# The first stage of an attention kernel put in a fixed order, with query and key halves sent through DRAM

## The chip, the cores and the metric

The kernel runs on one core of one Trainium2 chip. The metric is the device time of one execution in microseconds (us). A core has five engines that run side by side and wait for one another with semaphores: TensorE (PE) for matrix products, VectorE (DVE), ScalarE (ACT) and GpSimd (POOL) for elementwise work, and SyncE (SP), which here does nothing but issue transfers (DMAs). [...] A DMA belongs to the queue of the engine that issues it.

## The reference, cut to what matters

The input has two sequences of 2048 tokens with 256 features. Four layers follow one another, each added to its input: a softmax attention, a gated mixing of features, a second attention without softmax, and the mixing again. Only the first, `_L0_attn_a_ref`, is touched by the change, and what is computed stays the same:

```python
x = L0_attn_a_x                       # (2, 2048, 256)
h = layernorm(x)
q = h @ Wq + bq                       # 16 heads of 16
k = h @ Wk + bk                       # 4 key heads of 16
v = h @ Wv + bv
scores = einsum('bghnd,bhsd->bghns', q, k)      # 4 groups x 4 key heads
attn = softmax(scores / SCALE)        # SCALE = 4
out = einsum('bghns,bhsd->bghnd', attn, v)
x = x + out @ Wo + bo
```

## The kernel before, in words

The 4096 tokens lie in eight blocks of 512 (`NB = 8`), four for each sequence. `load(j)` prepares one block: it normalizes the tokens, turns them (`turn`, eight PE transposes), and makes keys (`pk`), queries (`pq`, two products of 128 rows, m = 0 and 1) and values (`pv`). Queries go to `qT`, values to `vA`, both with the bias already added.

Score products take their operands in a shorter float format. So that nothing is lost, each key and query is split into a high half (`kh`, `qh`: a cast) and a low half (what the cast left over: `kf`, `ql`, a subtraction on POOL). Keys and queries of one head, with their halves, are laid out over 64 partitions, so that one product sums all combinations. Laying them out is the task of `spread`: sixteen DMAs of 16 rows and 32 KB each, from SBUF to SBUF, for one block of keys (`kP`) or for one unit's queries (`qP`). For the first blocks it uses the queues of SP, POOL and ACT in turn.

A unit is one block of queries with one of four groups: 32 units of 16 key blocks (kb) of 128 keys. `project(u)` casts the query halves for two units at a time (when g is even) and lays them out. There are two `qh` and two `ql` buffers, and three sets of `qP`.

The softmax needs the largest score of each row before it can form exponentials, so `largest()` runs ahead: 64 steps for each unit, in each step one product of 128 x 512 scores (L300) and one maximum over it on DVE (L304). The look-ahead leads by `LEAD = 64 + 16` steps when the main loop begins. After a unit's 64 steps `turn_maxima` transposes the maxima and sends them to `mrows`.

The main loop then does for each key block: four look-ahead steps, four score products (L477), four products that subtract the maximum (L481), four exponentials on ACT (L485), and the four products with the values of the key block before (L464). `finish` closes a unit: sums and outputs go through DMAs (L385 to L395), DVE inverts the sums (L392), and after four units the output product is added to the tokens. There too the output bias is added to the tokens, on POOL (L378, once for each block of tokens).

What is in the program's text between the start and the main loop is not kept in that order. A scheduler places the instructions on each engine by its own estimate of when they can run; an instruction with nothing to wait for may move far ahead. `spaced` and the round counter in the text only decide in which order the instructions are offered to it. Later stages of the kernel use a helper, `in_order`, that ties each instruction to the one before it on its engine.

## Time and profile before

| | us |
|---|---|
| median of three runs (2225.53 to 2232.43) | 2229.49 |
| profiled execution | 2234.2 |
| its span, first to last instruction | 2232.1 |
| PE busy in it | 2171.0 |
| DVE busy in it | 1736.7 |
| ACT busy in it | 1421.4 |
| POOL busy in it | 361.4 |
| mean granted clock of PE | 0.987 |

An engine is busy while it executes an instruction; waiting, and issuing DMAs from SP and ACT, does not count. PE's products overlap, so a busy PE is not a PE at its peak. The granted clock is the share of full speed that the chip allows PE. A wait is put down to the engine or DMA whose signal came last.

### The profile page before, as it was taken

The page shows a single profiled execution, that of the slowest core. Times are in us where ns is not written, and L with a number is a line of the kernel's source. Part 1 is how long each engine was busy: PE and PEld are TensorE (multiplying, and loading weights), DVE is VectorE, ACT ScalarE, POOL GpSimd, SP SyncE. Part 2 cuts the span into 40 slices and gives each one's busy share as a digit, 9 for nine tenths or more (in the row PEclk, how much of TensorE's full clock was granted, in tenths as well). Part 3 has the DMA queues.
Part 4 walks back from the last instruction along what each step waited for, and adds up shares of the span by engine and source line. Part 5 has one row for each costly group of instructions (what it writes and reads, how often), then busy time and mean ns, then how long its engine had stood idle before and what let it go on. Part 6 is the DMA issues. An engine that isn't in the chain of part 4 may idle for free.

```text
span 2232.1 us, 39785 instructions
## 1 busy us (share of the span) xinstructions
PE 2171.0 (97%) x14426; PEld 1047.4 (47%) x14426; DVE 1736.7 (78%) x3339; ACT 1421.4 (64%) x2746; POOL 361.4 (16%) x337
## 2 busy tenths in 40 slices
PE   5999999999999999999999999999999999999998
PEld 2444444444444444444444444444343567676434
DVE  6758998988898899889889889989135588886335
ACT  2137777777777777777777777777864444554442
POOL 6310000000000000000000000000036245541450
PEclk9889999999999999999999999999999999999999
DMA  5111000100011000110001000100100000000002
GB/s 145 34 26 54 16 20 20 23 16 16 16 23 24 16 16 19 23 22 16 16 22 25 17 16 17 25 20 6 46 5 1 1 1 1 2 1 1 0 0 76
DMA packets 49779, 47.29 MB, mean 21 GB/s; under 512 B 25264, under 2 KB 34224, under 8 KB 49328
## 3 DMA queue, kind: packets, MB, share of 16 engines
q1 hardware_dynamic: 46944, 41.93, 7.8%
q8 instruction: 114, 1.87, 0.4%
q10 hardware_dynamic: 1360, 1.91, 0.3%
q0 software_dynamic: 1280, 0.92, 0.2%
q14 instruction: 81, 0.66, 0.1%
HBM read 14.29 MB, written 4.72 MB: 9 GB/s over the span
## 4 chain that ended last, share of the span: by engine, by line
PE 84%; DVE 7%; SPq 3%; DMA 1%; ACT 1%; issue 1%; POOL 1%; ACTq 0%; DVEq 0%; POOLq 0%
PE av L464 20%; PE s L300 17%; PE p L477 11%; PE q1f L653 7%; PE p L481 7%; DVE mx L304 4%; PE q2f L663 4%; PE pe L941 2%; PE po L407 1%; PE bpo L967 1%; SPq L389 1%; PE pw L811 1%; PE pq L254 1%; PE pq L802 1%; PE pv L811 1%; SPq L216 1%
## 5 line engine op out<-in xcount | busy, mean ns | idle before, releaser
L304 DVE TENSOR_REDUCE mx<-s 128x1 f32<-128x512 f32 x2048 | 1274.4, 684 | 135.5 <-PE s L300 131.8
L485 ACT ACTIVATE e<-p 128x512 f32<-128x512 f32 x2048 | 1061.3, 605 | 364.2 <-PE p L481 357.3
L300 PE MATMUL s<-a_kP,qP 64*128 64x512 f32 x2048 | 724.5, 473 | 16.2 <-DVE mx L304 14.3
L481 PE MATMUL p<-a_m,a_pick 64*128 64x512 f32 x2048 | 590.5, 418 | 0.0
L300 PEld LDWEIGHTS s<-a_kP,qP 64*128 64x128 f32 x2048 | 290.1, 185 | 587.4 <-DVE mx L304 552.1
L464 PE MATMUL av<-e,a_v 128*32 128x512 f32 x4096 | 548.0, 606 | 0.0
L477 PE MATMUL p<-qP,a_kP 64*128 64x512 f32 x2048 | 534.5, 398 | 2.0 <-ACT e L485 1.9
L477 PEld LDWEIGHTS p<-qP,a_kP 64*128 64x128 f32 x2048 | 287.7, 186 | 54.7 <-ACT e L485 27.0
L481 PEld LDWEIGHTS p<-a_m,a_pick 64*128 64x128 f32 x2048 | 285.0, 185 | 41.5 <-issue 3.0
L653 PE MATMUL q1f<-zq,wf 128*128 128x512 f32 x384 | 175.5, 600 | 0.0
L401 POOL TENSOR_TENSOR oc<-oc,sums 128x512 f32<-128x512 f32 x16 | 20.6, 1286 | 807.2 <-DMA sums<-dr 567.2
L464 PEld LDWEIGHTS av<-e,a_v 128*32 128x32 f32 x4096 | 81.0, 108 | 128.9 <-issue 120.3
L654 ACT ACTIVATE a1f<-q1f,wf 128x512 f32<-128x512 f32 x96 | 66.0, 689 | 99.5 <-PE q1f L653 96.1
L653 PEld LDWEIGHTS q1f<-zq,wf 128*128 128x128 f32 x384 | 70.6, 190 | 98.0 <-issue 86.4
L280 POOL TENSOR_TENSOR ql<-zq,qh 128x512 f32<-128x512 f32 x16 | 20.4, 1278 | 471.8 <-DMA dr<-rs 295.3
L663 PE MATMUL q2f<-a1f,wf 128*128 128x512 f32 x192 | 90.7, 617 | 0.0
L947 DVE TENSOR_TENSOR en<-pe,small 128x512 f32<-128x512 f32 x128 | 79.4, 683 | 12.3 <-PE pe L941 12.0
L692 DVE TENSOR_SCALAR cf<-cf,f_beta,alphaf 128x512 f32<-128x512 f32 x32 | 33.6, 1051 | 53.9 <-ACT cf L691 53.7
L696 POOL TENSOR_TENSOR tf<-cf,zq 128x512 f32<-128x512 f32 x32 | 56.1, 1752 | 93.6 <-DVE cf L692 93.2
L665 ACT ACTIVATE a2f<-q2f,wf 128x512 f32<-128x512 f32 x48 | 32.7, 688 | 56.0 <-PE q2f L663 56.0
L663 PEld LDWEIGHTS q2f<-a1f,wf 128*128 128x128 f32 x192 | 35.8, 196 | 45.9 <-issue 44.9
L698 POOL TENSOR_TENSOR zq<-zq,tf 128x512 f32<-128x512 f32 x32 | 56.8, 1775 | 2.5
(187 smaller groups left out, 1712.7 us busy)
## 6 DMA issues: line engine op xcount, KB each, us to landing
qP<-qh SPq DMA_DIRECT2D x256, 32.0 KB
qP<-ql SPq DMA_DIRECT2D x248, 32.0 KB
xs<-in_x SPq DMA_DIRECT2D x8, 512.0 KB
oc<-avs SPq DMA_DIRECT2D x128, 32.0 KB
sums<-dr SPq DMA_DIRECT2D x128, 32.0 KB
out<-xs SPq DMA_DIRECT2D x16, 256.0 KB
a_m<-mr SPq DMA_DIRECT2D x128, 4.0 KB
rope<-in_const SPq DMA_DIRECT2D x1, 2048.0 KB
```

The source lines that it names most:

```text
L300: mm(s, qP[r // 2][row, qi * P : (qi + 1) * P], kP[r // 2][row, k0 + kb * BLK : k0 + (kb + 1) * BLK], start=True, stop=True,)
L304: nc.vector.tensor_reduce(mx[:, qi, r : r + 1, kb], s, AX.X, ALU.max)
L464: mm(av[32 * r : 32 * r + 32, :], vA[:, units[u][0] // BPB * KB + kb, 32 * r : 32 * r + 32], es[r], start=(kb == 0), stop=(kb == KB - 1),)
L477: mm(t[r], kP[r // 2][row, k0 : k0 + P], qP[r // 2][row, :], start=True, stop=False)
L481: mm(t[r], pick[row, :], mrow[r // 2][row, :], start=False, stop=True)
L485: nc.scalar.activation(es[r], t[r], AF.Exp, scale=1.0 / HD**0.5)
L653: mm(q1, w1[:, c, m * P : (m + 1) * P], z[:, c, :], start=(c == 0), stop=(c == 1))
L654: nc.scalar.activation(a1[:, m, :], q1, AF.Gelu, bias=b1[:, m : m + 1])
L663: mm(q2, w2[:, c, :], a1[:, c, :], start=(c == 0), stop=(c == 1))
L696: nc.gpsimd.tensor_tensor(t1, cs, z[:, 0, :], ALU.mult)
L698: nc.gpsimd.tensor_tensor(z[:, 1, :], z[:, 1, :], t1, ALU.subtract)
L947: nc.vector.tensor_tensor(self.ens[t][w], pes[w].rearrange("p (h n) -> p h n", h=4), const("triu").unsqueeze(1).to_broadcast([P, 4, P]), A ...
```

## The change

1. Everything from the start to the end of the lead is listed step by step, and `in_order` ties all five engines, SP included, to that order. `spaced` and the rounds are gone. Blocks 0 and 1 are taken as far as the first queries and keys, then `pieces` hands out what is left of the blocks, one piece after every third look-ahead step, and later one for each key block of the main loop instead of every second.
2. `spread` is gone. `stored` writes the two halves to a DRAM tile in four DMAs (each half twice), with the rows in the order in which they are needed, and `fetch` reads two tiles of 128 rows from it. For queries four writes serve two units (256 KB each). All are issued by SP. For block 0 the halves are made by DVE straight from PSUM (`halve`), also for the first queries.
3. Value weights are packed without gaps (64 columns instead of 128). The value tile is set to 1.0 by POOL beforehand and ACT copies the values into it. The value bias is folded into the row that is added to the tokens (`bo_row`).
4. Loads: the constants come in three pieces, the token blocks 4 to 7 are issued after the first queries, and key and query biases are loaded by SP. The statistics of a block (`look`) are separate from its normalization, which moves from DVE to ACT (`scale`).
5. Two in five look-ahead steps of unit 0 take their PSUM bank from the other pool. The addition of `bo_row` to the tokens is kept at its place in the program.

The diff, cut to its core:

```diff
+    def in_order(first, which=(engines.PE, engines.DVE, engines.Activation, engines.Pool)):
+        last = {}
+        for ins in nc.cur_bb.bb.instructions[first:]:
+            if ins.engine in which:
+                if ins.engine in last:
+                    tc.add_manual_dep(
...
+                last[ins.engine] = ins
...
             def rows():
...
                 for of, e, to in heads:
                     nc.sync.dma_start(wo[to : to + 16, :, :], dwo[of : of + 16, :, e, :])
+                    at = _WA["bv"][0] + of
+                    nc.sync.dma_start(bv[to : to + 16, :], wa_d[0:1, at : at + 16].rearrange("o p -> p o"))
                 nc.sync.dma_start(bo, wa_d[:, slice(*_WA["bo"])])
+                yield
...
-            def spread(to, of, queues):
-                n = 0
-                for r in range(KV):
-                    for c, half in enumerate(of):
-                        at = 64 * (r % 2) + 16 * c
-                        queues[n % len(queues)].dma_start(
-                            to[r // 2][at : at + 16, :].bitcast(F32), half[16 * r : 16 * r + 16, :]
-                        )
-                        n += 1
+            def halve(hi, lo, product, bias):
+                if product is None:
+                    nc.vector.tensor_copy(hi, lo)
+                    nc.gpsimd.tensor_tensor(lo, lo, hi.bitcast(F32), ALU.subtract)
+                else:
+                    nc.vector.tensor_scalar(hi, product, bias, None, ALU.add)
+                    nc.vector.scalar_tensor_tensor(lo, product, bias, hi.bitcast(F32), ALU.add, ALU.subtract)
+                return lo
+
+            def stored(parts, rows, order):
+                d = dram.tile([4 * rows, BLK], F32, tag=f"d{rows}", name=f"d{rows}")
+                for at, i in enumerate(order):
+                    nc.sync.dma_start(d.rearrange("(p a) n -> p a n", a=4)[:, at, :], parts[i].bitcast(F32))
+                return d
+
+            def fetch(to, d, first):
+                for p in range(2):
+                    nc.sync.dma_start(to[p].bitcast(F32), d[first + P * p : first + P * (p + 1), :])
...
+            def look(j):
+                looks[j] = scales(lambda t: xs[:, 4 * j + t, :], f"a{j}")
+
+            def load(j, ld):
                 z = ld.tile([P, 4, D], F32, tag="z", name=f"z{j}")
-                normalize(z, lambda t: xs[:, 4 * j + t, :], f"a{j}")
-                yield
+                scale(z, lambda t: xs[:, 4 * j + t, :], *looks.pop(j))
...
+                kl = halve(kh, kf, pk[0:64, :] if j == 0 else None, bk)
+                d = stored((kh, kl), 64, (0, 0, 1, 1))
+                fetch([kP[p][:, j * BLK : (j + 1) * BLK] for p in range(2)], d, 0)
                 yield
...
+                        mm(
+                            pv[:, t * 64 : (t + 1) * 64], zb[c][:, t * P : (t + 1) * P], wv[:, c, :],
+                            start=(c == 0), stop=(c == 1),
+                        )
+                nc.scalar.copy(
...
             def project(u):
                 j, g = units[u]
                 if g % 2 == 0:
+                    if u > 0:
+                        qf = qT[:, g // 2, j * BLK : (j + 1) * BLK]
+                        qh = sb.tile([P, BLK], F32R, tag="qh", name=f"qh{u}", bufs=2)
+                        nc.vector.tensor_copy(qh, qf)
+                        ql = sb.tile([P, BLK], F32, tag="ql", name=f"ql{u}", bufs=2)
+                        nc.gpsimd.tensor_tensor(ql, qf, qh.bitcast(F32), ALU.subtract)
+                        halves[j] = qh, ql
+                    halves[j] = stored(halves[j], P, (0, 1, 0, 1))
                 qP = [sb.tile([P, BLK], F32R, tag=f"qP{p}", name=f"qP{u}_{p}", bufs=3) for p in range(2)]
-                spread(qP, [t[rows_g, :] for t in halves[j] * 2], [nc.sync, nc.gpsimd] if u == 0 else [nc.sync])
+                fetch(qP, halves[j], 2 * P * (g % 2))
...
+                        pool, tag = (psp, "p") if first and (4 * qi + r) % 5 > 2 else (pss, "s")
...
+                    tc.keep_in_program_order(
+                        nc.gpsimd.tensor_tensor(
+                            tokens(j), tokens(j), bo_row.unsqueeze(1).to_broadcast([P, 4, D]), ALU.add
+                        )
+                    )
...
+            arrive(0)
...
+            for r in range(KV):
+                nc.sync.dma_start(bk[16 * r : 16 * r + 16, :], wa_d[32 * r : 32 * r + 16, slice(*_WA["bk"])])
+            arrive(1)
...
+            arrive(2)
+            arrive(3)
+            blocks = [load(j, ld) for j in range(NB)]
+            look(0)
+            compact(wk, wkb, nc.scalar.copy)
+            look(1)
+            next(blocks[0])
+            compact(wq, wqb, nc.vector.tensor_copy)
+            next(blocks[0])
+            next(blocks[0])
+            project(0)
+            next(blocks[1])
+            next(blocks[1])
+            look(2)
+            look(3)
+            project(1)
+            at = slice(P, _CONST["mhalf"][0])
+            nc.sync.dma_start(small[:, at], consts[:, at])
+            for j in range(BPB, NB):
+                arrive(j)
+            compact(wv, wvb, nc.vector.tensor_copy)
+            more = rows()
+            next(more)
+
+            def memsets():
...
+                for j in range(NB):
+                    nc.gpsimd.memset(vA[:, 4 * j : 4 * j + 4, :], 1.0)
+
+            def pieces():
+                for j in (2, 3):
+                    for _ in range(2):
+                        next(blocks[j])
+                        yield
+                memsets()
+                look(4)
+                for j in range(BPB):
+                    for _ in blocks[j]:
+                        yield
+                for j in range(BPB, NB):
+                    if j + 1 < NB:
+                        look(j + 1)
+                    for _ in blocks[j]:
+                        yield
+                    if j == BPB:
+                        next(more)
+
+            rest = pieces()
+            LEAD = 64 + 16
+            for n in range(LEAD):
                 next(ahead)
+                if n % 3 == 1:
                     next(rest, None)
+                for f in later:
+                    f()
+                later.clear()
+            in_order(begin, (engines.PE, engines.DVE, engines.Activation, engines.Pool, engines.SP))
...
-                if kb % 2 == 0 and rest is not None and next(rest, "end") == "end":
+                if rest is not None and next(rest, "end") == "end":
```

## The prediction

> **What bounds the kernel now.** I read the page first (share of the span, slices), then the waits of TensorE (PE), then the start of the run in the windows and the timeline, because the change lies there.
>
> ```profile
> span 2232.1 us, 39785 instructions
> ...
> PE 2171.0 (97%) x14426; PEld 1047.4 (47%) x14426; DVE 1736.7 (78%) x3339; ACT 1421.4 (64%) x2746; POOL 361.4 (16%) x337
> ...
> PE   5999999999999999999999999999999999999998
> ...
> PEclk9889999999999999999999999999999999999999
> ```
>
> PE is busy 97% of the span. Time can come only from PE's work, its 61 us of idle time, or stretches at a lower granted clock. The clock row shows such a stretch in slices 2 and 3.
>
> ```profile
> 80.00:90.00 10.00, 8.76 (x23) 2.93 (x22) 8.63 (x15) 1.47 (x3) 2.54 (x2) 1.00 0.06 13
> 90.00:100.00 10.00, 7.13 (x15) 3.38 (x15) 10.00 (x12) 0.00 (x0) 10.00 (x5) 0.50 0.03 7
> 100.00:120.00 20.00, 19.41 (x58) 9.49 (x57) 12.74 (x26) 3.70 (x7) 5.32 (x3) 0.74 0.11 23
> 120.00:140.00 20.00, 18.48 (x56) 8.11 (x54) 17.59 (x32) 3.54 (x6) 4.87 (x3) 0.86 0.14 31
> 140.00:160.00 20.00, 19.95 (x97) 9.61 (x95) 3.12 (x6) 10.46 (x20) 2.55 (x2) 0.80 0.12 25
> ```
>
> The columns are PE, weight loads, DVE, ACT and POOL busy, clock, DMA share, GB/s. From 90 to 160 us the clock is 0.50, 0.74, 0.86, 0.80. At two states, full and half, that is 10 + 10.4 + 5.6 + 8 = 34 us at half rate, or 17 us lost where PE has work. The timeline (start, duration) shows what precedes it:
>
> ```profile
> 38.77 0.49 PE L300 MATMUL s<-a_kP,qP 64*128 64x512 f32 x1
> ...
> 87.46 11.88 POOL L378 TENSOR_TENSOR xs<-xs,a_bo_row 128x1024 f32<-128x1024 f32 x5 [18.85 <-DVE a_bo_row L207]
> ...
> 94.79 6.29 DVE L130 TENSOR_SCALAR z<-xs,mv_a,rs_a 128x256 f32<-128x256 f32 x4
> ...
> 197.96 0.40 PE L477 MATMUL p<-qP,a_kP 64*128 64x512 f32 x2
> ```
>
> The first score step of the look-ahead is at 38.8 us. At 87 us five of the eight bias additions of L378 run on POOL, long before they are needed, and beside them four normalizations take 6.29 us, which take 1.4 us elsewhere (timeline). PE waits, the clock falls. Unit 1 of the main loop begins at 197.96 us; I call all before it the front. The waits of PE in the front and in the main loop (198 to 1600 us) are, in us in all, times, longest:
>
> ```profile
> PE tr L137 <- DVE z L130: 23.9, 4, 20.6
> PE pv L262 <- ACT zq L255: 3.0, 2, 2.6
> PE s L300 <- DVE mx L304: 2.0, 4, 1.0
> ...
> PE s L300 <- DVE mx L304: 12.3, 36, 1.3
> ```
>
> So the front's 198 us are 20.6 of start, 8.3 of later waits, 17 of half rate, and the rest, 152, is PE work at full clock. In the main loop an undisturbed key block takes 2.71 us in the timeline, of which four reductions on DVE take 2.48; PE stalls only where DVE is held up.
>
> **The change, part by part.**
>
> *Start of the front.* Tokens 0 arrive at about 5 us in both. Statistics: 1.4 + 0.37 + 0.3 us on DVE, 1.2 on POOL, then four scalings on ACT (0.6, then 0.5 each, from L367), last at 10.3. Transposes and their copies end at 11.7, the key product at about 14.5, its halves (two DVE passes of 0.7 from PSUM) at 16. Before, DVE walked through the statistics of all eight blocks first (15 to 20 us) and PE began at 20.6. Then the halves go through DRAM. A write to DRAM and its landing is seen here:
>
> ```profile
> 210.27 0.52 SPq L393 DMA_DIRECT2D dr<-rs  x1
> 211.91 1.72 SPq L395 DMA_DIRECT2D sums<-dr  x4
> ```
>
> The reader of dr is issued 1.64 us after its writer. The page "DMA: Bandwidth & Descriptors" of the Trainium skill (Anatomy of one DMA) speaks against the change: a fixed 2.0 us for each DMA plus bytes over 436 GB/s, heaviest to HBM, so two in series cost twice what one does. By the row the trip costs 1.64 plus the data (the outputs at the end write 125 GB/s at a 0.37 share, so some 340 GB/s when full), by the rule 0.4 us more for each leg. SP issues keys (4 writes, 2 reads), then queries (4 writes, 2 reads), about 0.6 us each, each read waiting for its writes. By the rows: keys written by 18.6, read by 22; queries written by 25, read by 28.5 to 29.5; by the rule 1.6 us later. I take 29.5 for the first step: 9 us earlier than 38.8. But PE does only blocks 0 and 1 meanwhile: two transposes (1.03 each), two key products (1.93), one query product (1.9), 7.8 us of work. Its idle start is 29.5 - 7.8 = 21.7 us, against 20.6 now: the start itself gains nothing.
>
> *From the first step to unit 1.* The same 152 us of PE work. Value products have 64 instead of 128 columns, but each keeps its weight load (0.12 us; eight matmuls of two passes are 2.05 us now, at least 1.86 then): minus 1. DVE loses the normalizations (32, 17.9 us) and the value additions (8 x 0.685), and gets the query casts of all units: listing ends at the lead, so the scheduler pulls project's casts (L307) forward as soon as qT is there; in the built order nine stand before the main loop and six in its first eight key blocks, 0.43 each, up to 1.44 beside POOL. For the 80 lead steps DVE has 80 x 0.62 + four looks x 2.1 + casts, halves and bias 8 = 66 us, PE 75: PE is the longer. The eight additions of L378 stay at their place in the main loop, where reductions ran beside them at 4.87/8 = 0.61 us, so undisturbed: cost nothing; without that cover 8 x 2.4 = 19 us. The scalings on ACT (8 x 2.1 us) and the value copies lie in ACT's idle time (41.6 us before zb alone); ACT and POOL no longer issue key pieces, so ACT's waits for those (10.3 us before zq) and PE's 3.0 behind them go. On POOL the mask memsets (4 x 0.52) and eight new ones of the value tile (at most as long each, by their size) come after the key halves of block 3, some 6.5 us, against about six steps until the first value copy needs them: just covered, and within the 8 us of waits taken below where not. Two in five steps of unit 0 use the four banks of the other pool, so DVE can fall further behind before PE stops. Blocks 6 and 7 finish at one piece for each key block instead of every second; the weights of the later stages load sooner, and nobody waits for them.
>
> *What queues.* All transfers go through SP in order, and eight completion semaphores in rotation make each issue wait for the eighth before it. The key writes of block 2 stand behind seventeen small loads of Wo, bv and bo and the last 2 MB of tokens; 4-byte rows like these took 5 us to land. I get the keys of block 2 at about 58 us, needed for step 32 at about 57: a small wait. A cast needs the buffer of the cast before the last, freed when four 256 KB writes have landed: 1.28 (POOL half) + 2 (issue) + 1.64 + 0.75, some 6.5 us, longer behind a key read. Casts come every 4 us on average, two buffers allow 8; where two or three stand close, DVE stops, with the reductions behind it, and PE after three banks. Bounds: 0 to 20 us of PE idle; I take 8 with the waits of looks and key reads.
>
> *Clock.* "TensorE: Matmul & The Clock Gate" (What's actually happening) says that one busy window of 3.4 us restores full rate. The row shows PE dense from 101 us and 0.74 for the whole of 100 to 120, so half rate for 10 us more. By the rule an idle stretch costs PE under 2 us, by the row 5 to 10. I follow the row: 17 us are there to be won, and one new stall longer than a window would take back 5 to 10. I keep 3.
>
> Sum of the front: 21.7 + 151 + 8 + 3 = 184, against 198: minus 14. Bounds: no waits beyond 4 and full clock, 177; 15 of waits and 15 of half rate, 204.
>
> *Main loop after unit 1.* Before, each unit's sixteen 32 KB query pieces take SP 10 us, and the softmax sums queue between them. DVE, in order, waits for both:
>
> ```profile
> DVE rs L392 <- DMA rs<-ds: 27.7, 15, 17.9
> ...
> DVE qh L278 <- issue: 3.1, 8, 0.7
> DVE mx L304 <- PE p L477: 2.2, 2, 1.1
> DVE qh L278 <- DMA qP<-qh: 1.9, 3, 1.2
> ```
>
> Without the single 17.9, at the end where DVE has no reductions, that is 9.8 + 5 us, and each cast adds 0.34. PE lost 12.3 to reductions that came late. Now the casts are gone from here and two reads replace sixteen pieces, so the sums leave at once. I take 11 of the 12.3; bounds 4 (another DMA becomes late) and 12.3. The work behind attention is untouched.
>
> Together minus 25. The profiled execution took 2234.2 us (span 2232.1 and 2.1 around it): 2209. The median of the runs is 4.7 lower, 2229.5; from there 2204.5, so I say 2205.
>
> **Rivals.**
> *Casts choke the lead (slower).* The casts' buffers and SP's order decide: with twelve casts at 4 us spacing and two buffers, the cover ends at 8 us from cast to landing. Each us beyond it costs 12 x 0.5 = 6 us. At 12.5 us (a key read of 3 us and its writes stand before each set, landing near 2 us) that is 27 and the gain is gone; at 15 us it is 42: 2247. For it: SP's single order and sixteen new sets of 1 MB (four times 128 rows of 2 KB). Against: DMA share was 0.1 to 0.4. Chance 0.08.
> *Only the main loop gains.* The front keeps stalling: half rate comes back with a stall at block 2 or at a cast; front 194 to 200, main loop minus 11: about 2217. Chance 0.22.
> *The front runs clean.* 177 and the full 12.3: 2196. Chance 0.25.
> *Nothing to see.* The reads of 512 KB delay the sums as the pieces did and the front gains little: within 6 us. Chance 0.06.
>
> **How the numbers follow.** Chances: main case 0.39 (2198 to 2211), clean 0.25, main loop alone 0.22, nothing 0.06, slower 0.08. A measurement of this kernel tells about 0.3%, 6.7 us, from no change. The three gaining cases give 0.86 faster, 0.06 the same, 0.08 slower. The range 2189 to 2223 takes in the clean case and the main loop alone with their spread, and leaves out the last two and a little.
>
> **What would show it.** First L332 step at 29.5 us, not 38.8. Unit 1 beginning near 184 us. Clock 0.9 or more between 60 and 160 us; no additions of L411 before the main loop. DVE's waits for rs (L426) and for query casts after 180 us near zero, and PE's wait for reductions there under 2 us. I am wrong if DVE waits at L307 for more than 15 us in all, if PE waits for keys of block 2 or 3, or if the first step comes later than 34 us.

## The result, and the profile after

The kernel after takes 2191.86 us (median of 4 runs, 2187.96 to 2195.94) against 2227.91 us before: ratio 0.9836, 95% interval 0.9808 to 0.9864. Measured a second time on another occasion (`e10_after_again` below), the ratio was 0.9844, 0.9829 to 0.9858. So it is 1.6% faster, 36 us, where 25 were forecast. The profiled execution took 2194.6 us, its span 2192.8.

The page of after, first its busy times, then its 40 slices:

```profile
span 2192.8 us, 39103 instructions
...
PE 2141.5 (98%) x14430; PEld 1035.7 (47%) x14430; DVE 1715.5 (78%) x3310; ACT 1435.7 (65%) x2785; POOL 344.9 (16%) x311
...
PE   6999999999999999999999999999999999999998
...
PEclk8999999999999999999999999999999999999999
```

PE still bounds the kernel. Its idle time is 51 us now (2192.8 less 2141.5) and was 61. Its busy time fell by 29.5 us although it issues four matmuls more: that is the larger part, and the reader should wonder at it, because no product has left the program. The low slices 2 and 3 of the clock are gone from the row, and slice 1 is low instead; but slices of 55 us hide short stretches. The windows show them (PE, weight loads, DVE, ACT, POOL busy, clock, DMA share, GB/s):

```profile
60.00:80.00 20.00, 19.02 (x79) 9.42 (x77) 16.07 (x35) 6.65 (x12) 4.84 (x4) 0.94 0.67 217
80.00:90.00 10.00, 9.27 (x38) 4.43 (x36) 6.90 (x12) 3.40 (x7) 1.46 (x2) 0.96 0.60 178
90.00:100.00 10.00, 6.55 (x22) 3.94 (x23) 7.74 (x25) 2.76 (x6) 5.36 (x5) 0.83 0.55 211
100.00:120.00 20.00, 18.30 (x70) 8.50 (x70) 15.06 (x34) 9.71 (x19) 6.23 (x6) 0.91 0.54 157
120.00:140.00 20.00, 20.00 (x126) 9.73 (x125) 12.58 (x24) 12.53 (x25) 5.11 (x4) 1.00 0.90 317
```

From 60 to 120 us the clock dips a little in each window, where before it lay at 0.50 to 0.86 from 90 to 160. The timeline of the start, PE and SP's queue:

```profile
20.59 0.83 SPq L234 DMA_DIRECT2D a_kP<-d  x2
21.52 0.38 SPq L229 DMA_DIRECT2D d<-qh  x1
...
22.96 0.78 SPq L229 DMA_DIRECT2D d<-ql  x1
27.18 0.80 SPq L234 DMA_DIRECT2D qP<-d  x2
...
29.84 0.80 PE L332 MATMUL s<-a_kP,qP 64*128 64x512 f32 x2 [9.11 <-DMA qP<-d]
```

The reads of the keys are issued at 20.6, the last write of the queries at 23.0, their reads at 27.2, and the first score product runs at 29.84 us. Unit 1 of the main loop begins at 175.1 us in the timeline, 197.96 before.

The waits (us in all, times, longest), first in the main loop (175 to 1560 us), then DVE's for the casts in the front:

```profile
DVE rs L426 <- DMA rs<-ds: 22.7, 13, 16.5
...
PE s L332 <- DVE mx L336: 5.2, 22, 0.6
```

```profile
DVE qh L307 <- DMA d<-qh: 0.9, 1, 0.9
```

PE's waits for late reductions fell from 12.3 to 5.2 us. What is left on DVE at L426, without the 16.5 of the end, is 6.2 us of 9.8. The casts wait 0.9 us for their buffers, so the lead is not held up by them.

### The profile page after: what moved, and what is told of

It is laid out like the page before. It is cut to its first block, busy times and chain, and to the rows that moved or that the text cites. A ratio compares the mean times of both kernels' runs of the same rounds, so it can differ in the third digit from the quotient of the medians.

```text
span 2192.8 us, 39103 instructions
## 1 busy us (share of the span) xinstructions
PE 2141.5 (98%) x14430; PEld 1035.7 (47%) x14430; DVE 1715.5 (78%) x3310; ACT 1435.7 (65%) x2785; POOL 344.9 (16%) x311
## 4 chain that ended last, share of the span: by engine, by line
PE 89%; DVE 6%; ACT 2%; DMA 1%; issue 1%; POOL 1%; SPq 1%; ACTq 0%; DVEq 0%; POOLq 0%
PE av L534 22%; PE s L332 20%; PE p L547 10%; PE q1f L710 7%; PE p L551 7%; DVE mx L336 4%; PE q2f L720 4%; PE pe L998 2%; PE po L441 2%; PE pq L274 1%; PE bpo L1024 1%; PE pw L868 1%; PE pq L859 1%; PE pv L868 1%; PE q3f L730 1%; PE pk L859 1%
## 5 line engine op out<-in xcount | busy, mean ns | idle before, releaser
L332 PE MATMUL s<-a_kP,qP 64*128 64x512 f32 x2048 | 704.2, 471 | 15.3 <-DMA qP<-d 9.1
L332 PEld LDWEIGHTS s<-a_kP,qP 64*128 64x128 f32 x2048 | 281.3, 184 | 571.0 <-DVE mx L336 527.3
L547 PE MATMUL p<-qP,a_kP 64*128 64x512 f32 x2048 | 526.9, 393 | 2.6 <-ACT e L555 2.0
L435 POOL TENSOR_TENSOR oc<-oc,sums 128x512 f32<-128x512 f32 x16 | 20.6, 1286 | 1243.9 <-DMA sums<-dr 1093.6
L710 PE MATMUL q1f<-zq,wf 128*128 128x512 f32 x384 | 175.5, 600 | 0.0
L1004 DVE TENSOR_TENSOR en<-pe,small 128x512 f32<-128x512 f32 x128 | 79.3, 681 | 12.3 <-PE pe L998 12.1
L753 POOL TENSOR_TENSOR tf<-cf,zq 128x512 f32<-128x512 f32 x32 | 56.6, 1767 | 90.5 <-DVE cf L749 90.1
L754 DVE TENSOR_TENSOR zq<-zq,tf 128x512 f32<-128x512 f32 x32 | 22.1, 692 | 37.0 <-POOL tf L753 37.0
```

The source lines that it names most:

```text
L332: mm(s, qP[r // 2][row, qi * P : (qi + 1) * P], kP[r // 2][row, k0 + kb * BLK : k0 + (kb + 1) * BLK], start=True, stop=True,)
L547: mm(t[r], kP[r // 2][row, k0 : k0 + P], qP[r // 2][row, :], start=True, stop=False)
L710: mm(q1, w1[:, c, m * P : (m + 1) * P], z[:, c, :], start=(c == 0), stop=(c == 1))
L753: nc.gpsimd.tensor_tensor(t1, cs, z[:, 0, :], ALU.mult)
L1004: nc.vector.tensor_tensor(self.ens[t][w], pes[w].rearrange("p (h n) -> p h n", h=4), const("triu").unsqueeze(1).to_broadcast([P, 4, P]), A ...
```

## The experiments

To compare the kernels I use one account. The front (start to unit 1's first score product) is split three ways from the timeline and the granted clock: PE's work at full clock (busy time, with half of what lies in half-rate stretches taken off), what half rate cost (that half), and PE's idle time. The three add up to the front. The record of the clock begins only with its first change to full, at 25.2 us in before and 16.0 in after. Ahead of that the timeline shows after's transposes at half speed (seven in 2.31 us, later eight in 1.04), so in both kernels some 2 to 3 us of half rate at the start stand under work. Main is from there to the last score product of the last key block, tail the rest.

| kernel | median us | ratio, 95% | front | work | half rate | idle | main | tail |
|---|---|---|---|---|---|---|---|---|
| before | 2227.9 | 1 | 198.0 | 152.6 | 15.3 | 30.1 | 1411.8 | 622.4 |
| after | 2191.9 | 0.9836 (0.9808-0.9864) | 175.1 | 138.5 | 10.0 | 26.7 | 1399.1 | 618.6 |
| e1_bias_late | 2224.6 | 0.9979 (0.9972-0.9987) | 191.6 | 152.7 | 11.9 | 27.0 | 1408.8 | 621.7 |
| e2_store_only | 2230.5 | 1.0009 (1.0002-1.0017) | 200.5 | 153.3 | 15.1 | 32.1 | 1405.4 | 621.2 |
| e3_pieces | 2237.5 | 1.0036 (1.0028-1.0044) | 204.6 | 140.0 | 21.0 | 43.7 | 1411.5 | 622.6 |
| e4_no_order | 2184.9 | 0.9802 (0.9785-0.9820) | 161.5 | 134.9 | 2.7 | 23.9 | 1400.5 | 621.6 |
| e5_wide_values | 2190.1 | 0.9826 (0.9810-0.9842) | 171.1 | 138.4 | 6.6 | 26.2 | 1399.0 | 620.8 |
| e6_one_bank_pool | 2198.4 | 0.9865 (0.9848-0.9882) | 174.3 | 138.6 | 9.7 | 26.1 | 1399.2 | 621.0 |
| e7_order_but_PE | 2191.1 | 0.9829 (0.9814-0.9844) | 168.4 | 141.9 | 3.9 | 22.7 | 1398.8 | 622.8 |
| e8_order_but_DVE | 2199.5 | 0.9866 (0.9850-0.9883) | 178.6 | 138.1 | 12.7 | 27.9 | 1398.7 | 622.7 |
| e9_singles | 2230.6 | 1.0003 (0.9981-1.0025) | 207.2 | 149.4 | 33.0 | 24.8 | 1401.5 | 622.8 |
| e10_after_again | 2197.9 | 0.9844 (0.9829-0.9858) | 175.5 | 138.6 | 9.8 | 27.2 | 1399.9 | 620.9 |
| e11_order_three | 2193.9 | 0.9832 (0.9817-0.9847) | 169.2 | 139.5 | 5.6 | 24.2 | 1398.4 | 622.2 |
| e12_free_recip | 2178.6 | 0.9767 (0.9754-0.9781) | 162.1 | 135.3 | 2.9 | 24.0 | 1395.7 | 620.8 |

Ratios are to runs of before on the same occasion. The parts come from one profile each. How far a part can be trusted is seen from after and its repetition, and from the tails of kernels whose tails are alike: 618.6 to 622.8. Between kernels the half rate moves too: `e5_wide_values`, whose products cost what after's cost, has 3.4 us less of it. So a front that differs by 4 us or less from another kernel's proves little.

After's front is 22.9 us shorter than before's: 14.1 of work, 5.3 of half rate, 3.4 of idle time. Its main loop is 12.7 shorter. Each has its own cause.

**The bias additions at their place, alone** (`e1_bias_late`):

```diff
 if g == 0:
-    nc.gpsimd.tensor_tensor(
-        tokens(j), tokens(j), bo_row.unsqueeze(1).to_broadcast([P, 4, D]), ALU.add
+    tc.keep_in_program_order(
+        nc.gpsimd.tensor_tensor(
+            tokens(j), tokens(j), bo_row.unsqueeze(1).to_broadcast([P, 4, D]), ALU.add
+        )
     )
```

> The kernel before, with one edit: the eight bias additions on POOL (L378) are held at their place in the program, as in the change. Theory (the additions that ran beside the normalizations at 87 to 103 us made PE wait and brought on the half rate): four normalizations take 1.4 us again instead of 6.3, the half-rate stretch from 90 to 110 us goes or shrinks to one window; the front (start to unit 1) becomes 8 to 12 us shorter, 186 to 190, and the time about 2218. Rival (PE or the wait for DVE is the bound there in any case, and the clock falls at the next gap): front within 4 us of 198, time within 0.2% of before.

Measured: 0.9979, the front 6.4 us shorter, between theory and rival: 3.5 from half rate and 3.1 from idle time. One of the five additions still runs early on POOL. So the additions beside the normalizations are one real part of before's stall, a smaller one than expected. The half-rate stretch at 90 us shrinks from 20.5 to 10.2 us, but it begins as before, at 90.5 (90.0 in before, where the slow normalizations start only at 94.79). The additions lengthen this stretch; they don't bring it on. The one at 130 us, 13.7 us long, is still there.

**Queries through DRAM, alone** (`e2_store_only`):

```diff
-                    halves[j] = qh.bitcast(F32), ql
+                    halves[j] = (qh.bitcast(F32), ql) if u == 0 else stored((qh, ql), P, (0, 1, 0, 1))
...
-                spread(qP, [t[rows_g, :] for t in halves[j] * 2], [nc.sync, nc.gpsimd] if u == 0 else [nc.sync])
+                if u < 2:
+                    spread(qP, [t[rows_g, :] for t in halves[j] * 2], [nc.sync, nc.gpsimd] if u == 0 else [nc.sync])
+                else:
+                    fetch(qP, halves[j], 2 * P * (g % 2))
```

The rows of these queries come interleaved, while the keys keep their old order, so the scores are other numbers from unit 2 on; the amount of work is the same.

> The kernel before, with one edit: the query halves of units 2 and later go through DRAM (four writes for two units, two reads for one) instead of sixteen pieces from SBUF; keys and the first two units stay. Theory (in the main loop DVE waited for query casts and for the softmax sums behind the pieces on SP): from unit 1 to the end of the main loop 1411.7 us becomes about 1400, the wait of PE for reductions there falls from 12.3 to about 5; the casts move into unit 0, where they cost the front 0 to 4 us; time minus 8 to 12. Rival (the main loop gains from the order or the smaller PE work of the first stage, not from the pieces): main loop within 3 us of 1411.7.

Measured: the main loop 6.4 us shorter, the front 2.5 longer, and the time no better (1.0009). Half of the main loop's gain can be had in this way. The query casts move ahead with it: twelve of the sixteen run before unit 1 (three in before), the last at 218.2 us (1318.7 in before). So this edit changes the casts and the transfers together and doesn't tell the two apart.

**After with pieces instead of DRAM** (`e3_pieces`):

```diff
-                d = stored((kh, kl), 64, (0, 0, 1, 1))
-                fetch([kP[p][:, j * BLK : (j + 1) * BLK] for p in range(2)], d, 0)
+                spread([kP[p][:, j * BLK : (j + 1) * BLK] for p in range(2)], [kh.bitcast(F32)] * 2 + [kl] * 2, [nc.sync])
...
-                    halves[j] = stored(halves[j], P, (0, 1, 0, 1))
...
-                fetch(qP, halves[j], 2 * P * (g % 2))
+                rows_g = slice(64 * (g % 2), 64 * (g % 2) + 64)
+                hi, lo = halves[j][0].bitcast(F32), halves[j][1]
+                spread(qP, [t[rows_g, :] for t in (hi, lo) * 2], [nc.sync])
```

> The changed kernel with one part undone: keys and queries are laid out by sixteen SBUF pieces each, all on SP, instead of through DRAM. The listing and the rest stay. Theory (SP's issues are the price, 0.6 us each): first step near 38 us instead of 29.8, since keys and queries need 32 issues of 0.6; the front 8 to 20 us longer than 175.1; main loop from unit 1 back to about 1411; time plus 20 to 30. Rival (the trip through DRAM costs its latency and the bound lies elsewhere): first step 2 to 4 us earlier, front the same or shorter, time plus 5 to 12 by the main loop alone.

Measured: 1.0036, the whole gain gone, and more. The first step is not later (30.1 us), against the expectation. What follows it is: the queue of SP, where each piece takes 0.6 us, is behind from then on.

```profile
28.71 0.59 SPq L231 DMA_DIRECT2D qP<-qh  x1
29.34 0.59 SPq L231 DMA_DIRECT2D qP<-ql  x1
29.98 0.59 SPq L231 DMA_DIRECT2D qP<-qh  x1
30.61 0.59 SPq L231 DMA_DIRECT2D qP<-ql  x1
```

The front is 29.5 us longer than after's: 17 of idle time, 11 of half rate, 1.5 of work. The main loop is 12.4 longer, back at before's. So the layout through DRAM carries the main loop's whole gain in this kernel, together with the casts that it lets run ahead (the last is at 1325.7 us here, at 149.4 in after), and it is what lets one queue serve the front. Against before this run is not a single edit, since before used three queues for its pieces.

**After without the order** (`e4_no_order`); the listing stays:

```diff
-            in_order(begin, (engines.PE, engines.DVE, engines.Activation, engines.Pool, engines.SP))
```

> The changed kernel without the tie of the five engines to the listed order: the scheduler may move what is ready, everything else stays. Theory (the order is what brings the early scores: in the built order without it all statistics of blocks 2 to 7 stand before the first score maximum): first step 3 to 6 us later, front 5 to 12 us longer than 175.1; main loop from unit 1 unchanged within 2 us. Rival (the front's gain comes from DRAM layout, later loads and fewer value columns, not from the order): front within 4 us of 175.1.

Measured: 0.9802 (0.9785 to 0.9820), below the interval of after's second measurement (0.9829 to 0.9858), though it touches that of the first. The first step is 3.2 us later, as expected, and the front still 13.6 us shorter. My theory that the tied order makes the front's gain fell: the tie costs there. What after and this kernel share is the listing.

**Wide value weights** (`e5_wide_values`):

```diff
-            wv = hold.tile([P, 2, 64], F32, name="a_wv")
+            wv = hold.tile([P, 2, P], F32, name="a_wv")
...
-                            pv[:, t * 64 : (t + 1) * 64], zb[c][:, t * P : (t + 1) * P], wv[:, c, :],
+                            pv[:, t * P : (t + 1) * P], zb[c][:, t * P : (t + 1) * P], wv[:, c, :],
...
-            compact(wv, wvb, nc.vector.tensor_copy)
+            nc.vector.tensor_copy(wv.rearrange("p c m -> p (c m)"), wvb)
```

> The kernel after, but with the value weights left 128 columns wide with their gaps, as before, so that the 128 small value products of the front write 128 columns each instead of 64. Theory: the work of the matrix engine in the front came out some 13 us below the forecast, and the narrow value products are a part of it: their busy time was 21.8 us in the front of before and 16.0 us in that of after, so the wide ones give back 4 to 6 us in the front and nothing in the main loop (about 2197). Rival, the forecast's own term: the products cost about a slot each whatever their width, and the time rises by 1 us at most (2192 to 2193).

Measured: 0.9826, no different from after. The forms of the value products in the front, of this kernel, then of after (busy, mean ns of one):

```profile
L286 PE MATMUL pv<-a_wv,zb 128*128 128x128 f32 x128 | 16.4, 282 | 0.0
```

```profile
L286 PE MATMUL pv<-a_wv,zb 128*128 128x64 f32 x128 | 16.0, 278 | 0.0
```

Half the columns save 4 ns each. The rival held: before's 21.8 us for the same products were not their width. Half rate and their scattered places are what is left to explain them. Dropping the gaps is worth nothing measurable.

**One bank pool for unit 0** (`e6_one_bank_pool`):

```diff
-                        pool, tag = (psp, "p") if first and (4 * qi + r) % 5 > 2 else (pss, "s")
+                        pool, tag = pss, "s"
```

> The kernel after, but with unit 0's score products confined to the three banks of the score pool, as before, instead of two of five going to the other pool. Theory: the second pool is what lets score products of the two row halves follow each other closely (44.1 us busy for 146 of them in the front of after, 60.2 us in that of before); with three banks the product waits for the maximum that empties a bank, the waits for the maxima at L336 in the front rise from 0.5 us to 3 to 8 us, and the front grows by 4 to 10 us (2196 to 2202). Rival: the pairing comes from the order of the listing and not from the banks, and the time stays within 2 us of the kernel after (2190 to 2194).

Measured: 0.9865, with an interval that overlaps both measurements of after. PE's waits for the maxima in the front are 1.0 us, not 3 to 8, and front and work are after's within 1 us. The median lies in the theory's range, but no part of the profile carries it. The mechanism fell; whether the second pool is worth a few us stays open.

**Singles** (`e9_singles`). In after's listing one whole piece of a block stands behind each third score product. Here the same pieces are cut in three parts, one behind each score product:

```diff
 def load(j, ld):
...
-                turn(
-                    z, lambda c: psp.tile([P, BLK], F32, tag="p", name=f"tr{j}_{c}"),
-                    lambda c, tr: nc.scalar.copy(zb[c], tr),
-                )
+                for c in range(2):
+                    yield "part"
+                    tr = psp.tile([P, BLK], F32, tag="p", name=f"tr{j}_{c}")
+                    for t in range(4):
+                        nc.tensor.transpose(tr[:, t * P : (t + 1) * P], z[:, t, c * P : (c + 1) * P], ident)
+                    nc.scalar.copy(zb[c], tr)
                 yield
...
                     mm(pk[0:64, :], wk[:, c, :], zb[c], start=(c == 0), stop=(c == 1))
+                    yield "part"
...
                         mm(pq, wq[:, c, m * P : (m + 1) * P], zb[c], start=(c == 0), stop=(c == 1))
+                        yield "part"
...
                 for t in range(4):
+                    if t in (1, 3):
+                        yield "part"
...
             for n in range(LEAD):
                 next(ahead)
-                if n % 3 == 1:
+                if n > 0:
                     next(rest, None)
```

> The kernel after, with the same work in the front, but each piece of a token block (the turn, the key, query and value products) listed in three parts, one part behind each score product, instead of whole behind each third one; the written order is kept as before. So the score products of the front stand singly, as most did before (29 single and 15 pairs of 82, where after has 26 groups of three). Theory: the work of the matrix engine in the front fell by 14 us because products of the two row halves that stand next to each other run together: a group of three takes 0.73 us, a single one 0.50 us. Some 54 products that now stand singly then cost about 0.26 us more each: the work of the matrix engine before the main loop rises by 10 to 14 us, the front by 8 to 14 us (183 to 189 us), main loop and tail stay, 2199 to 2206 in all. Rival: the vector engine's reductions, 0.68 us each, set the pace, and a product hides in their time whether grouped or not: front within 3 us of 175, 2189 to 2195.

Measured: 1.0003, the whole gain gone, where the theory had 10 us or so. The work rises by 10.9 us, as the theory said; ahead of the main loop by 11.6, some 8 of them in the score products and the rest in the pieces that are cut up. Half rate costs 23.0 us more, which the theory had not seen. The score products ahead of the main loop, in before, after and this kernel (busy, mean ns of one):

```profile
L300 PE MATMUL s<-a_kP,qP 64*128 64x512 f32 x82 | 35.4, 530 | 1.4 <-DVE mx L304 0.8
```

```profile
L332 PE MATMUL s<-a_kP,qP 64*128 64x512 f32 x81 | 21.7, 492 | 9.1 <-DMA qP<-d 9.1
```

```profile
L338 PE MATMUL s<-a_kP,qP 64*128 64x512 f32 x82 | 40.4, 593 | 9.1 <-DMA qP<-d 9.1
```

Read busy against mean: 81 times 492 ns are 40 us of products in 21.7 us of busy time, so they overlap nearly two deep; in before 82 times 530 are 43 us in 35.4. The timeline shows why. Before, where pieces and steps were offered to the scheduler in turn:

```profile
69.38 0.71 PE L262 MATMUL pv<-wvb,zb 128*128 128x128 f32 x4
70.02 0.49 PE L300 MATMUL s<-a_kP,qP 64*128 64x512 f32 x1
70.44 0.71 PE L262 MATMUL pv<-wvb,zb 128*128 128x128 f32 x4
71.08 0.49 PE L300 MATMUL s<-a_kP,qP 64*128 64x512 f32 x1
```

and after:

```profile
60.37 0.72 PE L332 MATMUL s<-a_kP,qP 64*128 64x512 f32 x3
61.02 1.99 PE L274 MATMUL pq<-zb,a_wq 128*128 128x512 f32 x4
62.93 0.74 PE L332 MATMUL s<-a_kP,qP 64*128 64x512 f32 x3
63.60 2.00 PE L286 MATMUL pv<-a_wv,zb 128*128 128x64 f32 x16
```

From start to next start a single score product costs 0.42 us (70.44 less 70.02), a group of three 0.65 (61.02 less 60.37), or 0.22 each. Score products use one half of the rows. Two neighbours on different halves run at once (last section); with a product of full height between them, as in the rows of before, each pays its 0.42. Of 82 in the lead before had 29 singles and 15 pairs; after has 26 groups of three; this kernel has 42 singles and 17 pairs.

That is only about half of what before lost. From the start to unit 1, score products take 13.7 us of work less in after than in before (counted from start to next start at full clock). Singles and pairs, at 0.42 and 0.54 against 0.22 for each product in a group, explain some 7. The other 7 lie in two long runs of before, of 17 products from 85.2 us and of 11 from 129.7. The timeline has all but their first few in one row each:

```profile
88.03 7.68 PE L300 MATMUL s<-a_kP,qP 64*128 64x512 f32 x12 [0.44 <-DVE mx L304]
...
131.17 6.17 PE L300 MATMUL s<-a_kP,qP 64*128 64x512 f32 x10 [0.98 <-DVE mx L304]
```

Nothing stands between these products, and still they start 0.60 us apart (but for one step of 0.92), each some 0.04 us after a maximum has ended for which it waited. DVE, at 0.61 us for one maximum (eight in 4.87 us from 87.29), sets the pace, and PE is recorded as mostly busy while it waits. After has no such run; its listing puts pieces between the groups. No run takes this half away alone.

**After again** (`e10_after_again`), unchanged.

> The kernel after, unchanged, on the same chip as its variants of this call, with a second profile. Theory: the front, whose half-rate stretches differ between kernels that should be alike (17 to 27 us), is repeatable to 2 us in one and the same kernel (173 to 177 us), so that the difference of 13 us to the kernel without the written order is one of the kernels. Rival: stretches fall where they will, and the second profile's front differs by 5 us or more, which would make the order's cost smaller than the one pair of profiles said. Time 2188 to 2196.

Measured: front 175.5 against 175.1, with half-rate stretches at the same places within 0.2 us. The front belongs to the kernel, not to the run; the rival fell.

**Which engine's order costs** (`e7_order_but_PE`, `e8_order_but_DVE`, `e11_order_three`). Each changes the list of engines that are tied; in turn PE, DVE, or both are left out:

```diff
-            in_order(begin, (engines.PE, engines.DVE, engines.Activation, engines.Pool, engines.SP))
+            in_order(begin, (engines.DVE, engines.Activation, engines.Pool, engines.SP))
...
+            in_order(begin, (engines.PE, engines.Activation, engines.Pool, engines.SP))
...
+            in_order(begin, (engines.Activation, engines.Pool, engines.SP))
```

> The kernel after with the written order of the front kept on every engine and queue but the matrix engine, whose instructions the scheduler may place. The kernel with no order at all was 7 us faster, all of it in the front (161.5 us to unit 1's first score product instead of 175.1) with 5 us instead of 20 us of busy matrix engine at half rate. Theory: what the order costs is the matrix engine's, which waits with its next listed product for one late operand and then loses its full clock; here the front falls to 162 to 167 us with under 10 us of half rate, 2181 to 2187 in all. Rival: the order on the vector engine is the dear one, and the front stays within 3 us of 175 (2189 to 2193).

> The kernel after with the written order of the front kept on every engine and queue but the vector engine. The counterpart of the run without the matrix engine's order. If the matrix engine's order is what costs 13 us of the front, this one stays near the kernel after (front 172 to 177 us, 2189 to 2194). If the vector engine's order is (maxima and reductions held behind evacuations that wait), the front falls to 162 to 168 us here (2180 to 2187). If both are needed to free the front, both runs stay above 170 us.

> The kernel after with the written order of the front kept on the scalar engine, GpSimd and SyncE alone; the matrix and the vector engine may be placed by the scheduler. Without the matrix engine's order alone the front was 168 us, without the vector engine's alone 179 us, without any order 161.5 us. Theory: matrix and vector engine depend on each other (each reduction frees a bank for a product), so one order alone holds the other, and freeing both gives the whole 13 us: front 160 to 165 us, 2180 to 2187. Rival: the scalar engine's order (its evacuations in the listed place) is what costs, and the front stays at 168 us or more (2188 to 2197).

Measured: fronts of 168.4, 178.6 and 169.2 us, against 175.1 with all tied and 161.5 with none. Freeing PE takes off 6.7 us, near its theory's front though not its time: half rate and idle time fall by 10, while the work rises by 3.4, since the scheduler breaks up groups (17 singles in the lead, 1 in after). Freeing DVE alone gains nothing. Freeing both doesn't give the 13.6 us, so my theory fell there and the rival held: by these fronts the tie on ACT, POOL and SP is worth the other half. Which of the three it is wasn't run.

**Free order, and the reciprocal kept late** (`e12_free_recip`): the tie is gone as in e4, and

```diff
-                nc.vector.reciprocal(rs, rs)
+                tc.keep_in_program_order(nc.vector.reciprocal(rs, rs))
```

> The kernel after without the written order (as in the run that was 7 us faster), and with the reciprocal of the sums at L426 kept at its listed place, three or four key blocks later. What it is to tell: what is left of the main loop's loss. In the kernel after the vector engine waits 28.6 us in 14 waits at this reciprocal for the sums that come back from DRAM, and the key blocks behind it take 4.7 to 7 us longer in all than 2.71 us each. Theory: this wait is what the rest of the late reductions comes from; placed later it finds its sums, the excess falls below 2 us and the main loop by 4 to 6 us, to 1394 to 1397 us: 2177 to 2183 in all, the fastest of these kernels. Rival: the matrix engine does not wait for these reductions, or the later place delays the output projection: main loop stays at 1399 to 1402, 2183 to 2189.

Measured: 2178.58 us, 0.9767 (0.9754 to 0.9781), faster than before and after. The waits in the main loop are now

```profile
DVE rs L426 <- DMA rs<-ds: 16.7, 1, 16.7
...
PE s L332 <- DVE mx L336: 4.5, 20, 0.2
```

DVE waits at the reciprocal only at the end, PE's longest wait for a reduction falls from 0.6 to 0.2 us, and the main loop takes 1395.7 us, 4.8 less than e4's. Where a key block among numbers 3 to 7 of a unit took more than 2.71 us, the excess came to 14.9 us in all in before, 4.7 in after and 5.7 in e4; here it is 0.0. So what was left of this loss came from a reciprocal placed ahead of reductions, waiting for sums on their way back from DRAM.

## Why the prediction was right, and where only the sum was

*The first step* (29.5 forecast, 29.84 measured). The number held with some luck, since two errors met. The last query write was issued by 23.7 us, not 25, and from there to the first product 6.1 us went by where the row of the sums' round trip gave 3.5 to 4.5. So this time doesn't decide between that row and the rule of a fixed 2.0 us for each DMA (the Trainium skill, "DMA: Bandwidth & Descriptors", Anatomy of one DMA), which was worked out to put the step 1.6 us later; that section fits transfers issued by GpSimd, and these were issued by SyncE. PE's idle time in the front hardly changed, as said: 30.1 and 26.7.

*The front* (184 forecast, 175.1 measured, outside the bounds of 177 and 204). The gain of 14 was the right sign from the wrong terms:

| term of the front | forecast, before to after | measured |
|---|---|---|
| PE's work at full clock | 152 to 151 | 152.6 to 138.5 |
| half rate | 17 to 3 | 15.3 to 10.0 |
| start and waits | 28.9 to 29.7 | 30.1 to 26.7 |

The step that failed is "The same 152 us of PE work". It counted products and took a product's cost as fixed. Score products got 13.7 us cheaper instead. Some 7 of these are a matter of the neighbour: the listing puts three of them together, and e9, which takes this away and cuts the pieces for it, loses some 8 in them. The other 7 are the two runs of before that went at DVE's pace and were counted as PE work; that reading comes from the trace alone. The 1 us for narrow value products was about nothing (e5). The tie itself, to which the forecast gave no cost, costs 13.6 us of the front (e4).

*The clock.* Half rate was taken to come from the slow normalizations and the stall behind them, and to go with them. Some of it did (e1: 3.5 us of 15.3), but the clock of before falls at 90.0 us, within the run that goes at DVE's pace and ahead of that stall. Five stretches are left in after. For their length the forecast followed before's row (5 to 10 us lost) against the rule in "TensorE: Matmul & The Clock Gate" of the Trainium skill (What's actually happening: one busy window of 3.4 us restores full rate). In after the rule is the better one: behind the start there are four stretches of 3.4 us each. In before and in e9 it fails:

```profile
134.40:148.10 13.70, 13.69 (x32) 6.52 (x31) 5.73 (x11) 4.86 (x9) 2.52 (x2) 0.50 0.16 34
```

```profile
42.00:65.80 23.80, 23.80 (x44) 9.71 (x43) 11.09 (x24) 2.66 (x5) 10.11 (x19) 0.50 0.45 134
```

Here PE is recorded as busy throughout, and the clock stays at half for four and seven such windows. The first begins in the run at DVE's pace, the second lies where score products stand singly. Nor does half rate need a wait: in e9 it follows 3.4 us in which PE was recorded as busy all the time.

```profile
69.30:72.70 3.40, 3.40 (x21) 2.55 (x19) 2.54 (x4) 0.55 (x2) 0.00 (x0) 1.00 0.00 0
72.70:79.50 6.80, 6.80 (x9) 2.09 (x10) 2.23 (x5) 1.05 (x2) 0.00 (x0) 0.50 0.00 0
```

That grouping shortens half rate is shown by e9, 65.9 us of busy half-rate time against 20.0. Why is not: a single product at half rate is recorded for 0.79 us whatever the array does in it, so a busy record may hide an array that is little used, but no run measured that.

*The main loop* (minus 11 forecast, minus 12.7 measured). Casts gone and two reads for sixteen pieces: e3 gives the whole of it back, e2 has half. The cause was right, the account of it less so: of PE's 12.3 us of waits for reductions 11 were to go, and 7.1 went (5.2 are left, not under 2). What key blocks 3 to 7 took beyond 2.71 us fell by 10.2, so part of the gain was never in the recorded waits. DVE's waits at L426 are 6.2 us, not near zero; e12 takes these.

*The rivals.* "Casts choke the lead" needed waits of tens of us at L307; the row has 0.9. No addition of L411 runs ahead of the main loop: the first is at 141.3 us in the timeline. PE did not wait for keys of blocks 2 and 3. The clock was at least 0.9 where asked, but for 0.83 in one window of 10 us. In number the result is nearest to "the front runs clean" (2196), but the front was not clean: it lost 10.0 us to half rate, and its PE work fell instead.

*The sum.* For the profiled execution the forecast was 2209, and it took 2194.6. The 14.4 us are 8.9 of the front, 1.7 of the main loop and 3.8 of the tail, where nothing was forecast; in the second profile of the same kernel the tail is 1.5 below before's.

## What to carry to other kernels

Cost a product with its neighbours: where products use part of the array's rows, read busy time against count times mean, and look for the places where a full-height product stands between two that could run together; regrouping them is worth more than their widths. Before calling a run of equal products work, look at the distance of their starts: even steps as long as another engine's instruction are that engine's pace. List by groups first, and treat a tie of all engines to the list as an edit with a price of its own, to be run without. DVE did not pass over a reciprocal that waited for its DMA (e12 against e4: 4.8 us of the main loop); such an instruction belongs behind what the bound engine needs.

## What the hardware did that was not expected

A second score product on the other half of the rows is free. In e4's lead (timeline, start and duration) two take as long as one:

```profile
99.70 0.49 PE L332 MATMUL s<-a_kP,qP 64*128 64x512 f32 x1
...
101.13 0.50 PE L332 MATMUL s<-a_kP,qP 64*128 64x512 f32 x2
```

In after's lead such pairs start 3 to 7 ns apart. The Trainium skill says so ("TensorE: Matmul & The Clock Gate", Part 3, Measured speedup vs the span model: each further product in another part of the array adds about 4 ns to the first one's time); what it means for the order around them, the 8 us of e9, is this case's.

Half rate came behind waits shorter than itself. Ahead of the stretches of after that begin at 91.1 and 101.4 us stand single waits of 2.1 and 2.0 us:

```profile
PE a_pb L207 <- DVE a_db L205: 2.1, 1, 2.1
PE pm L352 <- DVE mt L347: 2.0, 1, 2.0
```

Both are shorter than the 3.4 us of a stretch. In the 3.4 us ahead of them PE was busy to 46% and 42%. But such waits don't always do it. In e7 PE is busy to 44% of 3.4 us, and the clock stays full there and in the 3.4 us behind:

```profile
92.90:96.30 3.40, 1.50 (x7) 0.70 (x7) 3.33 (x8) 0.77 (x2) 2.13 (x3) 1.00 0.65 249
96.30:99.70 3.40, 3.40 (x9) 1.15 (x10) 2.41 (x5) 0.69 (x1) 0.62 (x1) 1.00 0.83 192
```

In all these runs the half-rate stretches of the front last 3.41 us or a multiple of it, and within one run they begin on one grid of that step (in after at 22.86, 39.92, 77.47, 91.12 and 101.36 us). So what a wait costs may depend on where it falls in the grid; no run tested that.
